# Normalising later, batch-norm coefficients in pieces, and layer 3's norms on GpSimd in a planned four-layer graph network

## The chip, the cores and the metric

The kernel runs on one core of a Trainium2 chip. The metric is the device time of one execution in microseconds (us), taken as the median of several runs. TensorE (PE) multiplies matrices and writes PSUM, VectorE (DVE), ScalarE (ACT) and GpSimd (POOL) do the elementwise work, and SyncE's queue (SP) issues nearly all DMAs.

## The reference

All data are float32. The input x has 128 graphs of 64 nodes with 256 features, and one adjacency matrix serves all graphs. Four layers follow each other, each of the form x = layernorm(x + layer(x)), without gain or bias:

```python
# layer 0: aggregate, linear, batch norm over all rows, relu, linear, batch norm
agg = einsum('nm,bmd->bnd', A_hat, x)
h   = relu(batchnorm(agg @ W1.T + b1, g1, be1))          # 512 channels
out = batchnorm(h @ W2.T + b2, g2, be2)                  # 256 channels
# layer 1: einsum with a scaled Laplacian (power iteration for its largest eigenvalue),
#   @ Wc, layernorm, relu, residual; 4-head masked attention, layernorm; gelu MLP, layernorm
# layer 2: two graph convolutions, then LSTMs over windows of p = 1, 2, 3, 4 nodes,
#   each writing its last hidden state back before the next p
# layer 3: masked graph attention: Wh = x @ W, e = leaky_relu(s1 + s2), softmax, @ Wh
```

A batch norm needs the mean and the variance of each channel over all 8192 rows, so its second half can't begin before the last row of the first half is there. Layer 0 has two such points.

## The kernel before, in words

**Tiles.** The 8192 rows are 16 blocks of 512 rows (128 partitions x 4 tiles `t` of 256 features). `X[i]` holds block i's rows, and `H[i]` holds layer 0's second half of channels and later the LSTM's state. `PS` is a stock of four PSUM tiles of 128x1024, `mem` a stock of eight such tiles in SBUF (`t0` to `t7`), to which `X`, `H` and weight tiles are added when they are free. In the profile a tile's name says which storage a step borrowed, so one step has several names (`t<-`, `x<-`, `h<-`).

**Order.** The order of PE, DVE, ACT and POOL is not left to a scheduler. Each piece of work is a Python generator that yields `step(engine, us, ps, sl, waits, at, tbl)` ahead of the instructions of that step. `flow` keeps a clock for each engine ("T" PE, "V" DVE, "S" ACT, "G" POOL, "Q" the SP queue), and always emits the step that its estimates say can begin soonest; `ps` and `sl` are tiles taken, and `at` is a time before which a step is not ready. A margin, multiplied by a pseudo-random factor that the list `DRAWS` sets for each 50 us of planned time, shifts this choice. Streams hold tasks with a width (how many run at once) and a priority. So the estimates decide nothing about a time on the chip, but they decide every engine's instruction order, and each engine runs its instructions in that order. Steps marked `tbl="m"` on "V" wait in the plan for steps of "G" marked so.

**Layer 0.** `first_block(i)` aggregates a block (line 346), multiplies it by W1 in two halves of channels (`mm_fm`, line 370), lets ACT copy with the bias (line 589) and DVE take the statistics (`bn_stats`, line 593). When all 16 blocks are done, `bn_coeffs` aggregates the four channel groups (line 548), adds eps (549), takes the power -1/2 on POOL (551), and forms scale and shift (553 to 555). `second_block(i)` applies relu(scale*x+shift) on ACT (line 601, four passes a block) and multiplies by W2: block 0 plainly (line 611), the others with a Strassen-like scheme of seven products (line 645), whose sums are on DVE (636, 637, 641, 664 to 669), POOL (639) and ACT (656, 657, 675 to 677). Statistics follow (684), and `bn_coeffs` again.

**From layer 0 to layer 1.** `end_block(i)` loads x again (743), applies the batch norm on ACT (746), transposes on PE (364), adds the residual (DVE, 754), and normalises: `ln_steps_act` takes statistics of each 256-wide tile (`stats`, lines 290 to 292 on DVE), the power on POOL (313), minus mean times scale on DVE (316, `ln_nm`), and applies both with one ACT pass for each tile (319). `block(i)` is layer 1: it aggregates (346), multiplies (382), adds and normalises again (777, then lines 290 to 319), scales and adds (781 to 783 on DVE), transposes (358), and so on. The stream `seq` runs both, six at once; `ends` lists in which order end blocks run, and `at_end` how many of them are queued ahead of which block.

**Layers 2 and 3.** `gcn_block` and `unit` call `lstm`; its products are at lines 1081, 1153, 1289 and 1291, its differences T1 and T4 on POOL (1173, 1201). `last_block` is layer 3: for blocks 0 to 11 a whole block of four tiles, for 12 to 15 two halves of two tiles. It copies the state (1492), transposes, adds (1503), normalises with `ln_steps_act`, transposes (358), multiplies (1532), forms scores (1552 on POOL, 1556, 1557 on PE, 1561 to 1565 on DVE), takes the exponent on ACT (1569), divides (1571, 1572), multiplies (1578, 1588), adds (1599), normalises again with `ln_steps_act`, and stores (1603).

Of the kernel before, what the change touches and what calls it, by code (L numbers as in the profile page):

```python
# [15 lines left out]
P = 128  # L16
# [15 lines left out]
DRAWS = [511, 307, 323, 0, 388, 0, 0, 35, 178, 58, 461, 150, 363, 205, 36, 263, 190, 963, 453, 309, 108, 239, 50, 391, 578, 171, 630, 639, 804, 485, 290, 771, 646, 0, 976, 942, 0, 370, 0, 0, 618, 674, 887, 378, 432, 790, 44, 487, 800, 1]  # L32
# [3 lines left out]
def kernel(ctx: ExitStack, tc: tile.TileContext, a: dict, out: bass.AP):  # L36
# [79 lines left out]
    def mark(*key):  # L116
        done[key] = Clock.end
# [188 lines left out]

    def ln_steps_act(y):
# [6 lines left out]
        yield step("V", 0.2)  # L314
# [96 lines left out]
    with c0:  # L411
# [129 lines left out]
        def bn_coeffs(name, nch, st, g, be):  # L541

            mv = ctile([P, nch, 2], f"{name}mv")
            sc = ctile([P, nch], f"{name}sc")
            sh = ctile([P, nch], f"{name}sh")
            yield step("V", 0.15 + 0.5 * nch)
            for c in range(nch):
                V.bn_aggr(mv[:, c, :], st[:, c, :, :].rearrange("p i s -> p (i s)"))
            V.tensor_scalar(sc, mv[:, :, 1], EPS, None, ALU.add)
            yield step("G", 1.0)  # L550
            G.tensor_tensor(sc, sc, neghalf[:, :nch], ALU.pow)
            yield step("V", 0.6)
            V.tensor_tensor(sc, sc, g, ALU.mult)
            V.tensor_tensor(sh, mv[:, :, 0], sc, ALU.mult)
            V.tensor_tensor(sh, be, sh, ALU.subtract)
            bn[name] = sc, sh
            mark(name)
# [5 lines left out]
        def first_block(i):  # L563
# [6 lines left out]
            yield step("T", 0.95, ps=1, sl=1, tbl="quarter")  # L570
# [23 lines left out]
            mark("l0a", i)  # L594

        def second_block(i):
            sc1, sh1 = bn["bn1"]
# [5 lines left out]
            if i == 0:  # L603
                for f in range(4):
                    yield step("S", 0.7)
                    relu(f)
                    yield step("T", 1.75, ps=int(f == 0), waits=f == 3)
# [16 lines left out]
            yield step("S", 2.92)  # L624
            for f in range(4):
                relu(f)
# [4 lines left out]
            yield step("V", 1.4, sl=2, tbl="m")  # L631
# [5 lines left out]
            V.tensor_tensor(T2, h[:, :, v], T1, ALU.subtract)  # L637
            yield step("G", 1.3, waits=False, tbl="m")
            G.tensor_tensor(T4, h[:, :, u], T2, ALU.subtract)
            yield step("V", 0.7, tbl="m")  # L640
            V.tensor_tensor(T3, h[:, :, v], x[:, :, v], ALU.subtract)
# [8 lines left out]
            yield step("T", 1.75, ps=1)  # L650
# [4 lines left out]
            yield step("S", 0.75, waits=False)  # L655
            S.copy(y[:, 0, :], p[:, 0, :])
            S.copy(y[:, 3, :], p[:, 3, :])
            t = yield step("T", 1.75)
# [11 lines left out]
            yield step("T", 0.88)  # L670
# [3 lines left out]
            yield step("S", 1.5, ps=-1)  # L674
            S.activation(h[:, 0, :], fm(Xs[i])[:, 0, :], AF.Identity, bias=cols["b2"][:, 0:1])
            S.activation(h[:, 1, v], y[:, 3, :], AF.Identity, bias=cols["b2"][:, 1:2])
            S.activation(h[:, 1, u], p[:, 0, :], AF.Identity, bias=cols["b2"][:, 1:2])
# [3 lines left out]
        def second_stats(i):  # L681
            yield step("V", 1.25)
            for c in range(2):
                V.bn_stats(st2[:, c, i, :], H[i][:, c, :])
            mark("l0b", i)
# [4 lines left out]
        tasks.append(  # L690
            (
                lambda: ready(*[("l0a", i) for i in blocks]),
                lambda: bn_coeffs("bn1", 4, st1, cols["g1"], cols["be1"]),
                0,
            )
        )
        tasks += [(lambda: ready(("bn1",)), lambda i=i: second_block(i), 2) for i in blocks]
        tasks.append(
            (
                lambda: ready(*[("l0b", i) for i in blocks]),  # L700
                lambda: bn_coeffs("bn2", 2, st2, cols["g2"], cols["be2"]),
                0,
            )
        )
# [28 lines left out]
    sc2, sh2 = bn["bn2"]  # L733
# [3 lines left out]
    Wv_par = Wv.rearrange("p k (u r e) -> p k r u e", u=2, r=2)  # L737

    def end_block(i):
# [4 lines left out]
        yield step("S", 1.5)  # L744
        for c in range(2):
            S.activation(
                H[i][:, c, :], H[i][:, c, :], AF.Identity, scale=sc2[:, c : c + 1], bias=sh2[:, c : c + 1]
            )
# [8 lines left out]
        yield from ln_steps_act(x)  # L757
        mark("end", i)

    def block(i):  # L760
        x = X[i]
        mark("begun", i)
        yield step("T", 0.95, ps=1, sl=1, tbl="quarter")
# [68 lines left out]
        yield step("T", 0.95, ps=1, sl=1, tbl="quarter")  # L832
# [47 lines left out]
        yield step("T", 0.95, ps=1, sl=1, tbl="quarter")  # L880
# [156 lines left out]
    def lstm(p, n, parts, x_of, out_of):  # L1037
# [7 lines left out]
        us = n * 1.68e-3  # L1045
        v_us, g_us, s_us = (0.08 + n * r for r in (1.15e-3, 2.4e-3, 1.05e-3))
# [43 lines left out]
        def gates(pair, t, ps, sl):  # L1090
            t = yield step("S", 0.1 + n * 2.5e-3, ps=-1, at=t, waits=False)
# [56 lines left out]
        half_us, two_us = (0.15 + j * hn * 1.05e-3 for j in (1, 2))  # L1148
# [13 lines left out]
        for s in range(1, p):  # L1162
# [21 lines left out]
            def stage1(g):  # L1184
# [5 lines left out]
                at[g, "a"] = yield step("S", copy_us, at=t - us, waits=False)  # L1190
# [12 lines left out]
            def stage2(g):  # L1203
                v, y = places(g)
                yield step("T", us, at=h_at, waits=False)
# [8 lines left out]
            def stage3(g):  # L1214
# [3 lines left out]
                at[g, "0"] = yield step("V", two_us, at=at[g], waits=False)  # L1218
# [4 lines left out]
            def stage4(g):  # L1223
# [3 lines left out]
                yield step("S", 0.1 + n * 1.15e-3, at=at[g, "0"], waits=False)  # L1227
# [536 lines left out]
```

## Time and profile before

| | |
|---|---|
| median of 3 runs | 2354.76 us (2354.64 to 2355.97) |
| the profiled execution | 2355.12 us, of which the span is 2353.0 us |
| PE busy | 2266.4 us, 96% of the span |
| DVE, ACT, POOL busy | 58%, 50%, 19% |
| mean granted TensorE clock | 0.987 |
| chain that ended last | PE 80%, issue 8%, DVE 7%, ACT 4% |

The span runs from the first to the last instruction. A matmul in float32 shows as two records, so a product of 512 columns is two records of 0.43 us at the full clock. PEclk is the clock granted to TensorE as a share of the full one; a busy microsecond at 0.5 does half the work. A wait is put down to the instruction that came last before it.

### The profile page before, as it was taken

The page shows a single profiled execution, that of the slowest core. Times are in us where ns is not written, and L with a number is a line of the kernel's source. Part 1 is how long each engine was busy: PE and PEld are TensorE (multiplying, and loading weights), DVE is VectorE, ACT ScalarE, POOL GpSimd, SP SyncE. Part 2 cuts the span into 40 slices and gives each one's busy share as a digit, 9 for nine tenths or more (in the row PEclk, how much of TensorE's full clock was granted, in tenths as well). Part 3 has the DMA queues.
Part 4 walks back from the last instruction along what each step waited for, and adds up shares of the span by engine and source line. Part 5 has one row for each costly group of instructions (what it writes and reads, how often), then busy time and mean ns, then how long its engine had stood idle before and what let it go on. Part 6 is the DMA issues. An engine that isn't in the chain of part 4 may idle for free.

```text
span 2353.0 us, 40443 instructions
## 1 busy us (share of the span) xinstructions
PE 2266.4 (96%) x16916; PEld 1753.1 (75%) x16916; DVE 1365.9 (58%) x2865; ACT 1167.2 (50%) x2257; POOL 435.4 (19%) x322
## 2 busy tenths in 40 slices
PE   8989789999999999999999999999999999999996
PEld 4548666676666676667667888999988888978884
DVE  5557589666766556567544444454454655563567
ACT  2357465644454544445444444444444544653676
POOL 0011124221314224215120100011100111110112
PEclk9999899999999999999999999999999999999998
DMA  6100310000000000101000000000001001000111
GB/s 170 46 1 1 99 60 30 27 10 11 10 10 10 10 11 3 44 2 46 19 19 10 18 1 1 19 1 1 1 1 36 1 10 37 28 10 27 54 37 55
DMA packets 42632, 57.88 MB, mean 25 GB/s; under 512 B 6225, under 2 KB 35537, under 8 KB 42449
## 3 DMA queue, kind: packets, MB, share of 16 engines
q1 hardware_dynamic: 41344, 54.22, 7.2%
q8 instruction: 132, 2.16, 0.4%
q10 hardware_dynamic: 1104, 1.08, 0.1%
q14 instruction: 52, 0.42, 0.1%
HBM read 38.52 MB, written 16.78 MB: 23 GB/s over the span
## 4 chain that ended last, share of the span: by engine, by line
PE 80%; issue 8%; DVE 7%; ACT 4%; POOL 0%; DMA 0%; ACTq 0%; POOLq 0%; DVEq 0%
PE ps L1153 27%; PE ps L1081 14%; PE ps L370 11%; PE ps L382 6%; PE ps L945 4%; PE ps L645 3%; PE ps L346 2%; PE ps L815 2%; PE ps L1532 2%; PE ps L1289 2%; PE ps L1291 2%; PE ps L358 2%; DVE ln_st L290 1%; PE ps L364 1%; DVE ln_mv L291 1%
## 5 line engine op out<-in xcount | busy, mean ns | idle before, releaser
L1153 PE MATMUL ps<-t,x 128*128 128x256 f32 x928 | 226.8, 380 | 0.3 <-DVE x L1221 0.3
L313 POOL TENSOR_TENSOR ln_rs<-ln_rs,neghalf 128x4 f32<-128x4 f32 (+1 forms) x104 | 108.5, 1043 | 610.6 <-DVE ln_rs L292 535.6
L1153 PEld LDWEIGHTS ps<-t,x 128*128 128x128 f32 x928 | 173.0, 190 | 22.8 <-issue 1.6
L1049 ACT ACTIVATE t<-ps,bih 128x512 f32<-128x512 f32 (+5 forms) x185 | 98.2, 568 | 159.7 <-PE ps L1081 103.7
L319 ACT ACTIVATE x<-x,ln_nm,ln_rs 128x256 f32<-128x256 f32 x228 | 118.1, 591 | 66.9 <-DVE ln_nm L316 66.9
L1153 PE MATMUL ps<-x,x 128*128 128x256 f32 x608 | 147.5, 380 | 1.5 <-DVE t L1221 1.1
L1049 ACT ACTIVATE x<-ps,bih 128x512 f32<-128x512 f32 (+5 forms) x159 | 82.2, 548 | 106.3 <-PE ps L1081 67.9
L1153 PEld LDWEIGHTS ps<-x,x 128*128 128x128 f32 x608 | 114.4, 190 | 17.2 <-DVE t L1221 1.8
L370 PE MATMUL ps<-t,W1T 128*128 128x512 f32 x256 | 114.7, 595 | 0.0
L290 DVE BATCH_NORM_STATS2 ln_st<-x 128x6 f32<-128x256 f32 x244 | 97.6, 400 | 0.7
L1049 ACT ACTIVATE x<-x,bih 128x512 f32<-128x512 f32 (+5 forms) x134 | 69.3, 564 | 51.8 <-DVE x L1219 49.7
L1081 PE MATMUL ps<-t,wL 128*128 128x512 f32 x216 | 94.6, 594 | 0.2 <-ACT t L1378 0.2
L291 DVE BATCH_NORM_AGGREGATE ln_mv<-ln_st 128x2 f32<-128x6 f32 x448 | 81.4, 182 | 15.3
L1081 PE MATMUL ps<-h,wL 128*128 128x192 f32 (+2 forms) x456 | 89.6, 352 | 0.6 <-DVE x L1599 0.6
L1081 PE MATMUL ps<-h,x 128*128 128x256 f32 x384 | 86.1, 379 | 0.0
L370 PEld LDWEIGHTS ps<-t,W1T 128*128 128x128 f32 x256 | 46.7, 190 | 48.9 <-issue 48.5
L1081 PEld LDWEIGHTS ps<-h,wL 128*128 128x128 f32 x456 | 69.6, 190 | 17.8 <-issue 16.0
L1212 DVE COPY x<-ps 128x256 f32<-128x256 f32 (+2 forms) x67 | 25.5, 381 | 98.4 <-PE ps L1153 98.4
L1219 DVE TENSOR_TENSOR x<-ps,x 128x512 f32<-128x512 f32 (+2 forms) x67 | 40.8, 609 | 69.3 <-PE ps L1153 64.3
L316 DVE SCALAR_TENSOR_TENSOR ln_nm<-ln_mv,ln_rs 128x4 f32<-128x4 f32 (+1 forms) x104 | 61.4, 593 | 33.2 <-POOL ln_rs L313 33.1
L1081 PEld LDWEIGHTS ps<-h,x 128*128 128x128 f32 x384 | 72.8, 190 | 9.8
L319 ACT ACTIVATE t<-t,ln_nm,ln_rs 128x256 f32<-128x256 f32 x112 | 58.5, 591 | 41.0 <-DVE ln_nm L316 40.9
(692 smaller groups left out, 5374.3 us busy)
## 6 DMA issues: line engine op xcount, KB each, us to landing
t<-in_x_dram SPq DMA_DIRECT2D x28, 512.0 KB, 4.4
xd<-x SPq DMA_DIRECT2D x16, 512.0 KB, 2.6
x<-xd SPq DMA_DIRECT2D x8, 512.0 KB, 3.3
out_dram<-x SPq DMA_DIRECT2D x8, 512.0 KB, 2.9
wL<-in_L_gnn_Wih_dram SPq DMA_DIRECT2D x2, 1024.0 KB, 4.9
x<-in_L_gnn_Whh_dram SPq DMA_DIRECT2D x2, 1024.0 KB, 5.0
wB<-in_L_gnn_W_dram SPq DMA_DIRECT2D x2, 512.0 KB, 4.3
h<-in_x_dram SPq DMA_DIRECT2D x2, 512.0 KB, 4.0
```

Source lines behind the costliest of these rows:

```text
L290: V.bn_stats(st[:, t, :], y[:, t, :])
L291: V.bn_aggr(mv[:, t, :], st[:, t, :])
L313: G.tensor_tensor(rs, rs, neghalf[:, :n], ALU.pow)
L316: V.scalar_tensor_tensor(nm, mv[:, :, 0], -1.0, rs, ALU.mult, ALU.mult)
L319: S.activation(y[:, t, :], y[:, t, :], AF.Identity, scale=rs[:, t : t + 1], bias=nm[:, t : t + 1])
L370: T.matmul(ps[:, c, :], w[:, k, (off + c) * P : (off + c + 1) * P], yT[:, k, :], start=(k == 0), stop=(k == nk - 1),)
L382: T.matmul(ps[:, t, :], yT[:, k, t * P : (t + 1) * P], w[:, k, :], start=(k == 0), stop=(k == nk - 1),)
L645: T.matmul(dst, w[:, k, :], y[:, k, :], start=first and k == 0, stop=k == 1, skip_group_check=not first)
L945: T.matmul(tm(PS[ps])[:, t, :], fm(mem[gs[k // 2]])[:, k % 2, t * P : (t + 1) * P], W2[:, k, :], start=(k == 0), stop=(k == 3),)
L1049: S.activation(dst, z, AF.Tanh, bias=bl[:, p - 1, 2 * g + c : 2 * g + c + 1], scale=(1.0 if g == 2 else 0.5) * (1.0 if p == 1 else 0.5),)
L1081: T.matmul(spread(fm(PS[ps])[:, j, :n], q), WL[p][0][:, k, m], x_of(0, q)[:, k], start=(k == 0), stop=(k == 1),)
L1153: T.matmul(dst, WS[p][name](k, g), y[:, k], start=first and k == 0, stop=k == 1, skip_group_check=not first)
```

## The change

1. **Batch norm in pieces.** `bn_coeffs` works on a range of channel groups. For the first batch norm it is called twice, for groups 0 and 1 (written by the first half of `first_block`) and for groups 2 and 3. Each `bn_aggr` is a step of its own, ready when its group's statistics are complete. Block 0 of `second_block` begins with the first two groups; the other blocks wait for both.
2. **`second_block`** is cut into smaller steps: two relu passes, the difference T1, the first products, two relu passes, the other differences. The last block takes the statistics of its first channel group before its other ACT passes.
3. **Late norms.** `end_block` normalises block 0 alone; for the others the layer norm stands at the beginning of `block(i)`. Four end blocks, not two, are queued ahead of block 0.
4. **True waits on PSUM.** In `lstm` several steps get a later `at` (the time when the tile that they overwrite has been read), and many estimates are changed. `DRAWS` is another list.
5. **Layer 3's norms.** Both use a new `ln_steps_pool`: POOL takes the power, and then applies (y - mean) * rs in one `tensor_scalar` with two scalars of each partition for each tile. Line 316 and the four (or two) ACT passes of line 319 fall away there.

```diff
-DRAWS = [511, 307, 323, 0, ...]
+DRAWS = [438, 839, 188, 0, ...]
...
+    def ln_steps_pool(y):
+        n = y.shape[1]
+        yield step("V", 0.3 + 0.53 * n)
+        mv, rs = stats(y)
+        yield step("G", 1.0)
+        G.tensor_tensor(rs, rs, neghalf[:, :n], ALU.pow)
+        for t in range(n):
+            yield step("G", 0.7, tbl="m")
+            G.tensor_scalar(
+                y[:, t, :], y[:, t, :], mv[:, t, 0:1], rs[:, t : t + 1], ALU.subtract, ALU.mult
+            )
...
+        def bn_coeffs(name, c0, c1, st, g, be, at):
+            sc, sh, mv = (t[:, c0:c1] for t in bn[name])
+            for c in range(c1 - c0):
+                yield step("V", 0.5, at=lambda: at(c0 + c))
+                V.bn_aggr(mv[:, c, :], st[:, c0 + c, :, :].rearrange("p i s -> p (i s)"))
+            yield step("V", 0.2)
             V.tensor_scalar(sc, mv[:, :, 1], EPS, None, ALU.add)
             yield step("G", 1.0)
-            G.tensor_tensor(sc, sc, neghalf[:, :nch], ALU.pow)
+            G.tensor_tensor(sc, sc, neghalf[:, : c1 - c0], ALU.pow)
...
             if i == 0:
                 for f in range(4):
-                    yield step("S", 0.7)
-                    relu(f)
-                    yield step("T", 1.75, ps=int(f == 0), waits=f == 3)
+                    if f % 2 == 0:
+                        for j in (f, f + 1):
+                            t_j = yield step("S", 0.65, at=lambda: done.get(("bn1", f)))
+                            relu(j)
+                    yield step("T", 1.75, ps=int(f == 0), at=t_j - 0.65 * (1 - f % 2))
...
-            yield step("S", 2.92)
-            for f in range(4):
-                relu(f)
+            t_x = yield step("S", 1.46)
+            relu(0)
+            relu(1)
...
+        for c in (0, 2):
+            tasks.append(
+                (
+                    lambda c=c: stats_at(c),
+                    lambda c=c: bn_coeffs("bn1", c, c + 2, st1, cols["g1"], cols["be1"], stats_at),
+                    0,
+                )
...
+    NORMED = range(1)
...
         mem.give(xin)
-        yield from ln_steps_act(x)
+        if i in NORMED:
+            yield from ln_steps_act(x)
         mark("end", i)
...
     def block(i):
         x = X[i]
         mark("begun", i)
+        if i not in NORMED:
+            yield from ln_steps_act(x)
...
-                yield step("T", us, at=h_at, waits=False)
+                yield step("T", us, at=max(h_at, at[g, "a"], at[g, "e"]), waits=False)
                 product(g, "A12", h_u, v[:, 2, :])
...
-        yield from ln_steps_act(x)
+        yield from (ln_steps_pool if True else ln_steps_act)(x)
...
-    at_end = {0: 2, 1: 4, 2: 8, 3: 10, 4: 14, 5: 16}
+    at_end = {0: 4, 1: 4, 2: 8, 3: 10, 4: 14, 5: 16}
```

The line with `ln_steps_pool` stands twice, once for each of layer 3's norms.

## The prediction

> **What bounds the kernel now.** First the page: PE is busy 2266.4 of 2353.0 us, so only its idle time and its time at a reduced clock can be won. Where they lie, the table of stretches says (start:end, the length, busy time with instructions of PE, PEld, DVE, ACT, POOL, then the granted clock):
>
> ```profile
> 0.00:145.00 145.00, 136.34 (x1345) 74.89 (x1346) 75.59 (x159) 39.22 (x61) 2.51 (x15) 1.00 0.32 88
> 145.00:255.00 110.00, 99.49 (x421) 79.89 (x420) 70.90 (x125) 76.86 (x139) 21.35 (x16) 0.97 0.06 19
> 255.00:330.00 75.00, 54.69 (x427) 38.08 (x425) 53.73 (x137) 41.41 (x69) 13.47 (x15) 0.80 0.25 79
> 330.00:400.00 70.00, 66.97 (x744) 49.83 (x743) 58.93 (x120) 42.05 (x64) 33.51 (x19) 1.00 0.12 37
> 400.00:1750.00 1350.00, 1343.95 (x10599) 1018.93 (x10600) 766.63 (x1416) 636.42 (x1098) 283.39 (x171) 1.00 0.04 13
> 1750.00:2000.00 250.00, 238.53 (x1378) 213.42 (x1377) 134.62 (x291) 125.40 (x295) 28.73 (x26) 0.99 0.06 20
> 2000.00:2305.00 305.00, 297.72 (x1761) 258.09 (x1760) 168.44 (x481) 173.59 (x438) 41.62 (x44) 1.00 0.09 30
> 2305.00:2353.00 48.00, 28.73 (x252) 19.96 (x250) 37.02 (x142) 32.22 (x100) 10.81 (x16) 0.80 0.20 66
> ```
>
> Length minus PE busy is the idle time. The same table in slices of 5 us, with busy x (1 - clock) summed, gives what the reduced clock takes: 2.0 us in the second stretch, 9.8 in the third, 1.2 in the sixth, 2.7 in the last. Lost altogether: 8.7 us at the start, 12.5 around the first batch norm, 30.1 around the second, 3.0 and 6.1 in layers 1 and 2, 12.7 and 7.3 in the LSTM with layer 3, 22.0 at the end; 102 in sum. Next the waits of PE in the second and the third stretch (waited for, us, times, longest):
>
> ```profile
> PE ps L611 <- ACT x L601: 6.7, 1, 6.7
> PE ps L358 <- DVE ln_nm L316: 6.3, 1, 6.3
> PE ps L364 <- ACT h L746: 4.9, 2, 4.6
> PE ps L346 <- ACT x L319: 4.1, 1, 4.1
> ```
>
> The first is the first batch norm, the third the second one, the fourth the first layer norm of layer 1, the second a stall 25 us later. Last, in order of time, what stands in the 6.7 us:
>
> ```profile
> 149.90 1.29 DVE L593 BATCH_NORM_STATS2 st<-h 128x6 f32<-128x512 f32 x2 [2.15 <-ACT h L589]
> 151.10 1.91 DVE L548 BATCH_NORM_AGGREGATE bn1mv<-st 128x2 f32<-128x96 f32 x4
> 153.30 1.01 POOL L551 TENSOR_TENSOR bn1sc<-bn1sc,neghalf 128x4 f32<-128x4 f32 x1 [144.18 <-DVE bn1sc L549]
> 155.00 2.22 ACT L601 ACTIVATE x<-x,bn1sh,bn1sc 128x512 f32<-128x512 f32 x3 [4.55 <-DVE bn1sh L555]
> 155.86 5.77 PE L611 MATMUL ps<-x,W2T 128*128 128x512 f32 x8 [6.72 <-ACT x L601]
> ```
>
> PE stood from 149.15 to 155.86, and its next eight records took 5.77 us, where four of the same later take 1.88: the clock was 0.51 in that slice.
>
> **First batch norm.** The last x half has its statistics at 144.3, so groups 0 and 1 can be worked while PE still multiplies the last h halves. Two aggregations (0.48 each) give 145.3, line 549 (0.17) 145.5, POOL's power of 128x2 (0.70, as in the second batch norm) 146.3, three DVE operations 146.9, two relu passes 148.5, between ACT's copies at 145.75 and 149.18. These extra instructions (one line 549, one power, three DVE operations, 1.4 us) lie beside PE's products; without that cover they would cost their 1.4. Block 0's f = 0 and 1 are eight records of 0.43: PE works until 152.6. Groups 2 and 3 end at 151.2, and the same chain reaches the first relu's end at 154.5. The gap shrinks from 6.7 to 1.9 us, -4.8; a gap of 1.9 us at 165 left the clock at 1.00, so the 2.0 us go too. **-6.8.** The finer steps of the other blocks I cost at nothing: PE is bound there (1.03 us for four records, back to back), and the waits left (3.1 us on line 657) stay. Bounds -3 (the early chain queues behind DVE's statistics and ACT's copies, and reaches PE late) and -10 (those waits go too).
>
> **Second batch norm.** One aggregation (0.51 of 1.02 us) leaves the chain: -0.5. Two more end blocks are queued ahead of block 0. Each has two passes of ACT (0.8 each; ACT stands 5.5 us before 275.78), a transposition (3.46 us at half clock in this place, 1.95 at the full one), a DVE sum (1.22) and a load on SP's queue ahead of them; the loads were issued from 245 on. PE waits 4.1 us ahead of 276.44 and 1.1 ahead of 280.39: 5.2 us at half clock, 2.6 us of work that need not be done later. -2.6. Against it, two DVE sums stand ahead of `ln_nm`; they fit while POOL takes the power.
>
> The 6.3 us stall ended at 301.5. Ahead of it DVE did statistics of two later end blocks (292.96 to 297.6, 2.3 us each), then 3.7 us of lines 781 to 783 that PE needs; these were ready at 295.2, when ACT had normalised. With late norms both groups are gone: at least -2.6, and with the two sums of 290.62 already done -3.6; I take -3.1. The clock was at 0.66 from 300 to 315 and cost 4.2 of the 9.8 us; a gap half as long may or may not cause that (2.3 us at 2309.9 did), so half: -2.1. **Sum -8.3**, bounds -3 and -14.
>
> The moved norm brings its nine DVE instructions and `ln_nm`, POOL's power (1.0) and four ACT passes (2.1) to the head of `block(i)`, some 6 us; queued behind the wait on PE is only this block's aggregation, and five other tasks can run. Layers 1 and 2 lose 6.1 us in 1350, with DVE busy 57%, so nothing. If that cover were gone, 15 norms of 6 us would be 90 us, but then these rows would show idle PE. From 330 to 400 DVE is at 84%, and three to four norms leave or arrive there: 0, bounds -2 and +3.
>
> **LSTM and PSUM waits.** No instruction is added; the order is redrawn. 20.0 us are lost from 1750 to 2305, in single waits of at most 1.8 us, mostly on DVE and ACT. Later `at`s keep a product from standing in PE's queue ahead of work that is ready: -2, bounds -8 (half) and +10 (the redrawn order stalls half as much again).
>
> **Layer 3's norms.** 128 ACT passes (66.8 us busy by the table of line 319) and 40 `ln_nm` go; 128 passes come to POOL. No row has such a pass. One input of 256 elements: at least 0.40 (two inputs, 128x128, line 1552), at most 1.36 (two inputs, 128x512, line 639); nearest is 128x256 at 0.62, which I take: 79 us on a POOL that is busy 81 of 603 us. Latency: `ln_nm` 0.16, a hop and two passes of 1.09 against two of 0.62: even. But POOL in turn holds up DVE:
>
> ```profile
> 193.75 0.69 DVE L637 TENSOR_TENSOR t<-h,t 128x512 f32<-128x512 f32 x1
> 195.18 1.54 DVE L637 TENSOR_TENSOR t<-h,t 128x512 f32<-128x512 f32 x1
> 194.61 1.56 POOL L639 TENSOR_TENSOR t<-h,t 128x512 f32<-128x512 f32 x1 [4.50 <-ACT x L656]
> ```
>
> The second DVE sum ends 0.55 us after POOL's at 196.17: it waited. From 2305 on POOL would be busy 10.8 + 28 x 0.62 = 28 of 48 us, and DVE (32.1 of the 36 us from 2310) has 14 such operations (lines 1563 and 1572) and eleven of line 292 (0.25 on average over all 104 of four columns, most of them in layer 1 where POOL works more; 0.17 here): 25 x 0.58 x 0.31 (half a pass) = +4.5, less 2.1 for eleven `ln_nm`: +2.4. ACT loses 14.8 us there, but only part of PE's waits there name it: -1. **End: +1.4**, bounds -3 and, at 1.36, +12. Between 1750 and 2305 the same gives 100 passes, ACT relieved of 52 us, PE's waits on ACT (8.2 us) somewhat shorter and DVE's longer: 0, bounds -3 and +6.
>
> The page "SBUF — State Buffer" of the Trainium skill (section "SBUF: two separate sides") says more: a GpSimd operation and a DVE operation with two SBUF inputs share a port pair as an exclusive lock, and the loser stands for the whole instruction. The row above agrees; by that, with DVE standing for whole passes, the 4.5 would be 9.0, the end +5.9 and the sum -11.2. The page "GPSIMD Engine Reference" (section "Engine selection") speaks against this part: elementwise work belongs on VectorE, though with one input POOL is said to be roughly at line rate. By that, an estimate of 256 / 1.2 GHz = 0.21 us plus dispatch, a pass would lie near the lower bound, the end term near -1 and the sum near -18.
>
> **Sum.** -6.8 - 8.3 - 2 + 1.4 + 0 = -15.7. On the profiled execution's 2355.1 us (the span's 2353.0 and 2.1 around it) that is 2339.4; the median of the runs lies 0.4 lower: **2339 us**. This case's own range, adding up about half of each bound, is 2325 to 2350.
>
> **The rivals.** (a) *The early gain is given back.* The norms come back in 330 to 400, where DVE is at 84%, or the new gaps still reduce the clock: half of the 15.1 us, so 2346. For it: a gap of 2.3 us was enough once. Against: the norms of blocks 12 to 15, four times 2.6 us of DVE, move far away. (b) *The new order loses in the LSTM.* A different list of draws and other estimates reorder all 555 us; the slices of 50 us there range from 0 to 4 us lost. A loss as large again as the 20 now gives 2339 + 22 = 2361 at the worst, 2355 in the middle. Against: the steps now wait for what they really wait for. (c) *POOL becomes the bound of the end: slower.* If a pass costs over about 1.0 us, POOL has 10.8 + 28 = 39 of 48 us, DVE stands behind it, and each half block's two norms grow by 1 us or more. At 1.36: end +12, 1750 to 2305 +6 and T4 on POOL's queue behind passes +3, so 2360; it decides from 1.0 us on. For it: the power takes 0.70 for two elements, so not everything on POOL goes by size. Against: the row at 0.62. (d) *The pieces do nothing*: the order keeps the early coefficients behind the last copies, and the gaps stay: 2351.
>
> **How the numbers follow.** 0.2% (4.7 us) is about what a measurement can tell from no change. Forecast 0.58; (a) 0.12; (b) 0.11; (c) 0.14; (d) 0.05. Faster, below 2350.1: 0.57 + 0.10 + 0.03 + 0.01 + 0.01 = 0.72. Slower, above 2359.5: 0.03 of (b), 0.10 of (c) and 0.03 that several bad bounds meet, taken from forecast and (a): 0.16. The rest, 0.12, lies between. The range from 2325 to 2361 leaves out some 0.05 below, and 0.10 above from (c) and the tail of (b).
>
> **What would show it.** Line 611 starts within 3 us of line 370's last record; no slice there below clock 0.9. The wait on line 316 around 300 is under 4 us; the stretch that begins at the second batch norm loses about 22 us, not 30. POOL's new row has 128 instructions of 0.4 to 0.8 us. The last 48 us lose 19 to 24. A mean above 1 us in that row, or over 25 us lost in the LSTM, would make the prediction wrong.

## The result, and the profile after

The changed kernel takes **2345.34 us**, median of 5 runs (2343.41 to 2348.53), beside 2355.47 us for the kernel before on the same chip (2354.64 to 2355.97): a ratio of 0.9958, interval [0.9944, 0.9973]. It is 10.1 us faster where 16 were forecast. The profiled execution took 2343.84 us, of which the span is 2342.1 us. The time is inside the range, but two terms were wrong and nearly made up for each other.

The table of stretches, in the form shown before (PE, PEld, DVE, ACT, POOL, granted clock):

```profile
145.00:255.00 110.00, 103.77 (x448) 84.07 (x446) 79.46 (x142) 79.79 (x145) 22.38 (x18) 1.00 0.11 36
255.00:330.00 75.00, 61.94 (x767) 47.29 (x768) 49.04 (x108) 43.40 (x63) 15.71 (x15) 0.84 0.22 69
330.00:400.00 70.00, 68.60 (x560) 48.67 (x560) 49.41 (x92) 41.04 (x58) 28.50 (x16) 1.00 0.13 42
400.00:1750.00 1350.00, 1341.26 (x10523) 1024.44 (x10522) 753.41 (x1483) 651.42 (x1130) 287.51 (x176) 1.00 0.03 12
1750.00:2000.00 250.00, 239.68 (x1455) 216.07 (x1454) 134.69 (x308) 118.31 (x287) 72.94 (x61) 1.00 0.07 24
2000.00:2305.00 305.00, 289.39 (x1664) 247.18 (x1662) 167.21 (x460) 134.45 (x361) 139.21 (x123) 0.98 0.09 30
2305.00:2342.00 37.00, 19.71 (x170) 13.19 (x166) 21.49 (x82) 8.57 (x35) 30.28 (x31) 0.72 0.17 58
```

Around the first batch norm PE is idle for 6.2 us where it was 10.5, and the clock stays at 1.00. Around the second one it is idle for 13.1, not 20.3. At the bottom it is the other way round: POOL is now the busiest engine of the last stretch, 30.3 of 37 us, where DVE and ACT led before.

Fixed stretches cut the work of the two kernels at different places, so the ledger goes by milestones: when the last record of a kind starts, in us.

| | before | after | ahead |
|---|---|---|---|
| last product of layer 0 (line 645, now 660) | 262.9 | 251.6 | 11.3 |
| last plain LSTM product (line 1289, now 1322) | 2293.8 | 2273.4 | 20.4 |
| end of the span | 2353.0 | 2342.1 | 10.9 |

Up to the last plain LSTM product more is won than forecast (17.1); then 9.5 of the 20.4 us go in the last 69.

Over the whole span idle time and reduced clock together take 98.1 us, where they took 102.4. So only 4.3 of the 10.9 us were won there. The other 6.6 us are PE's busy time at the full clock, which became shorter with the same 16916 records; no view shows by what (the ends of records are modelled, and the clock is given to two digits). The prediction's opening, that "only its idle time and its time at a reduced clock can be won", does not hold for this profile.

The waits of PE in the first two of the stretches:

```profile
PE ps L377 <- ACT h L775: 5.9, 2, 5.0
PE ps L359 <- ACT x L332: 4.3, 1, 4.3
PE ps L371 <- DVE t L815: 3.3, 1, 3.3
PE ps L628 <- ACT x L616: 2.1, 1, 2.1
```

The last line is the first batch norm (6.7 before), the third the stall 25 us after the second one (6.3 before, then put down to `ln_nm`); the waits of the second batch norm itself have not shrunk (9.0 before in two lines, now 10.2). What stands around the 2.1 us, first on PE and then on ACT, in order of time:

```profile
151.97 3.70 PE L628 MATMUL ps<-x,W2T 128*128 128x512 f32 x8 [2.06 <-ACT x L616]
```

```profile
149.95 1.26 ACT L604 ACTIVATE h<-ps,l0b 128x512 f32<-128x512 f32 x2 [2.17 <-PE ps L383]
151.10 1.51 ACT L616 ACTIVATE x<-x,bn1sh,bn1sc 128x512 f32<-128x512 f32 x2
```

Scale and shift of groups 0 and 1 were ready at 147.6, and ACT then stood idle for 2.17 us, up to 149.95. But in ACT's order the last copies of the first pass (line 604) come ahead of the relu, and so the first product waits for both. Its eight records (two products, f = 0 and 1) take 3.70 us, at the full clock; before they took 5.77. No gap follows, since groups 2 and 3 are ready by 155.5.

In the end the chain of work that ended last runs on POOL (start, length, what):

```profile
2319.32 1.22 POOL h L316
2320.54 0.37 POOL t L1585
2320.91 1.20 POOL h L316
2322.11 1.00 POOL ln_rs L313
...
2324.45 1.22 POOL h L316
...
2327.22 1.21 POOL h L316
2328.43 0.69 POOL ln_rs L313
...
2329.22 2.53 POOL h L316 x2
```

From 2319 to the last pass at 2337.5 POOL goes from pass to power to pass. Its new row, the first of three for line 316, one for each kind of tile (shortest/median/longest in ns, first and last start in us), shows the price of a pass:

```profile
L316 POOL TENSOR_SCALAR x<-x,ln_mv,ln_rs x52: 1212/1220/2507, 1808.3 to 2334.1; 128x256 f32<-128x256 f32 x52
```

A pass takes 1.22 us, and by the groups 1.27 on average, held-up passes included (162.6 us in 128). The forecast took 0.62.

### The profile page after: what moved, and what is told of

Same layout as the page of the kernel before. It is cut to its first block, busy times and chain, and to the rows that moved or that the text cites. A ratio compares the mean times of both kernels' runs of the same rounds, so it can differ in the third digit from the quotient of the medians.

```text
span 2342.1 us, 40447 instructions
## 1 busy us (share of the span) xinstructions
PE 2260.4 (97%) x16916; PEld 1755.7 (75%) x16916; DVE 1330.5 (57%) x2829; ACT 1116.2 (48%) x2137; POOL 599.1 (26%) x451
## 4 chain that ended last, share of the span: by engine, by line
PE 77%; DVE 5%; POOL 3%; ACT 2%; issue 2%; POOLq 0%; DVEq 0%; ACTq 0%
PE ps L1186 26%; PE ps L1114 14%; PE ps L383 11%; PE ps L395 7%; PE ps L977 5%; PE ps L847 2%; PE ps L359 2%; PE ps L371 2%; PE ps L1565 1%; PE ps L1322 1%; PE ps L1324 1%; POOL h L316 1%; DVE ln_st L290 1%; PE ps L920 1%; PE ps L377 1%
## 5 line engine op out<-in xcount | busy, mean ns | idle before, releaser
L1186 PE MATMUL ps<-t,x 128*128 128x256 f32 x800 | 195.0, 380 | 0.0
L1082 ACT ACTIVATE x<-ps,bih 128x512 f32<-128x512 f32 (+5 forms) x201 | 102.9, 547 | 182.4 <-PE ps L1114 106.4
L326 POOL TENSOR_TENSOR ln_rs<-ln_rs,neghalf 128x4 f32<-128x4 f32 x64 | 74.1, 1158 | 432.0 <-DVE ln_rs L292 390.6
L1186 PE MATMUL ps<-x,x 128*128 128x256 f32 x704 | 171.9, 379 | 0.9 <-DVE x L1254 0.9
L1186 PEld LDWEIGHTS ps<-t,x 128*128 128x128 f32 x800 | 150.4, 190 | 20.5 <-issue 1.0
L1082 ACT ACTIVATE t<-ps,bih 128x512 f32<-128x512 f32 (+5 forms) x148 | 78.2, 566 | 136.5 <-PE ps L1114 85.7
L1082 ACT ACTIVATE x<-x,bih 128x256 f32<-128x256 f32 (+5 forms) x146 | 74.1, 558 | 47.9 <-DVE x L1252 47.8
L332 ACT ACTIVATE x<-x,ln_nm,ln_rs 128x256 f32<-128x256 f32 x152 | 78.7, 592 | 33.9 <-DVE ln_nm L329 33.9
L313 POOL TENSOR_TENSOR ln_rs<-ln_rs,neghalf 128x4 f32<-128x4 f32 (+1 forms) x40 | 38.3, 956 | 192.8 <-DVE ln_rs L292 176.8
L1252 DVE TENSOR_TENSOR x<-ps,x 128x512 f32<-128x512 f32 (+2 forms) x73 | 43.7, 600 | 62.5 <-PE ps L1186 55.5
L1114 PEld LDWEIGHTS ps<-t,wL 128*128 128x128 f32 x192 | 36.3, 190 | 44.7 <-issue 42.6
```

Source lines behind the costliest of these rows:

```text
L326: G.tensor_tensor(rs, rs, neghalf[:, :n], ALU.pow)
L332: S.activation(y[:, t, :], y[:, t, :], AF.Identity, scale=rs[:, t : t + 1], bias=nm[:, t : t + 1])
L1082: S.activation(dst, z, AF.Tanh, bias=bl[:, p - 1, 2 * g + c : 2 * g + c + 1], scale=(1.0 if g == 2 else 0.5) * (1.0 if p == 1 else 0.5),)
L1114: T.matmul(spread(fm(PS[ps])[:, j, :n], q), WL[p][0][:, k, m], x_of(0, q)[:, k], start=(k == 0), stop=(k == 1),)
L1186: T.matmul(dst, WS[p][name](k, g), y[:, k], start=first and k == 0, stop=k == 1, skip_group_check=not first)
```

## The experiments

Three questions: what POOL's passes cost and where; what each half of layer 0's change is worth; and what the new order alone does. One theory says that the end's loss of 9.5 us is POOL's long pass, its rival that it is the redrawn order. One thing stands in the way: whatever changes a step makes the plan draw every later choice anew. Six kernels therefore keep a planned order (the steps are announced as before, only the instructions behind them differ; PE's order is the same record by record), and the rest were planned anew. Beside all of them the kernel before took 2354.9 to 2355.2 us, so their times can be set beside the 2345.34 of the changed kernel.

### Which engine applies layer 3's norms

**Passes on ACT, planned anew** (`act`):

```diff
-        yield from (ln_steps_pool if True else ln_steps_act)(x)
+        yield from ln_steps_act(x)
```

> The changed kernel with layer 3's two norms applied by ACT again (ln_steps_act), all else as changed. Theory 1 (a POOL pass of 1.2 us makes POOL the bound of the end): the last 48 us lose about 22 us as before, not 37 to 41 us over the last 90, and the time is 2333 to 2338 us. Theory 2 (the end is longer because the whole order was redrawn, not because of POOL): 2343 to 2348 us, with the end as long as in the changed kernel.

Measured: 2333.23 us (2332.36 to 2333.97), ratio 0.9906 [0.9893, 0.992]. It beats both kernels: with layer 3's norms left on ACT, the rest of the change, in the order that came out of this plan, is worth 22 us. On PE the order is that of the changed kernel up to 1810 us.

**The changed kernel's order, passes on ACT** (`order_pool_act`):

```diff
         for t in range(n):
             yield step("G", 0.7, tbl="m")
-            G.tensor_scalar(
-                y[:, t, :], y[:, t, :], mv[:, t, 0:1], rs[:, t : t + 1], ALU.subtract, ALU.mult
-            )
+            if t == 0:
+                nm = sm.tile([P, n], F32, tag="ln_nm", name="ln_nm")
+                V.scalar_tensor_tensor(nm, mv[:, :, 0], -1.0, rs, ALU.mult, ALU.mult)
+            S.activation(
+                y[:, t, :], y[:, t, :], AF.Identity, scale=rs[:, t : t + 1], bias=nm[:, t : t + 1]
+            )
```

> The order of every engine as the changed kernel has it (the same planned steps), but in layer 3's norms the passes are emitted on ACT, with line 316's old product on DVE ahead of them. Only the engine differs. Theory 1 (POOL's passes of 1.2 us themselves cost the end): 2333 to 2338 us, 8 to 12 less than the changed kernel. Theory 2 (the order planned for POOL costs it): 2343 to 2347 us.

Measured: 2336.72 us (2335.62 to 2338.23), ratio 0.9923 [0.9909, 0.9937].

**`act`'s order, passes on POOL** (`order_act_pool`): the same exchange the other way round.

```diff
...
+        yield step("V", 0.2, tbl="m")
+        yield step("S", 0.1 + 0.5 * n)
+        for t in range(n):
+            G.tensor_scalar(
+                y[:, t, :], y[:, t, :], mv[:, t, 0:1], rs[:, t : t + 1], ALU.subtract, ALU.mult
             )
...
-        yield from (ln_steps_pool if True else ln_steps_act)(x)
+        yield from ln_steps_act_pool(x)
...
```

> The order of the kernel that had ACT do the norms in the changed plan (2333 us), but the passes are emitted on POOL. Theory 1: 2343 to 2350 us, 10 to 16 more. Theory 2 (it is the order): 2333 to 2336 us.

Measured: 2360.37 us (2357.5 to 2361.88), ratio 1.002 [1.0011, 1.0029]. That is 10 us above the dearer of the two theories; why POOL costs so much more in this order is not shown. The four together:

| | passes on POOL | passes on ACT | POOL costs |
|---|---|---|---|
| order planned for POOL | 2345.34 | 2336.72 | 8.6 |
| order planned for ACT | 2360.37 | 2333.23 | 27.1 |

In either order POOL is the slower place. In its own order it costs 8.6 us, and that is the exchange of the engine alone. Where in the span, the two profiles with the same order show; each row is the stretch from the last plain LSTM product to the end, first of the changed kernel, then of `order_pool_act`:

```profile
2273.40:2342.10 68.70, 42.34 (x310) 30.20 (x308) 41.66 (x147) 22.48 (x81) 51.76 (x50) 0.77 0.14 47
```

```profile
2271.70:2334.20 62.50, 43.51 (x310) 29.51 (x308) 42.43 (x159) 37.86 (x111) 12.58 (x18) 0.79 0.15 51
```

The same 310 records of PE stand behind the milestone in both. With POOL they take 68.7 us, with ACT 62.5: 6.2 of the spans' 7.9 us are lost here, the rest before. POOL is the busiest engine of its stretch (51.8 of 68.7 us), while with ACT no engine is above 43.5 of 62.5.

**Half blocks on ACT, whole blocks on POOL, same order** (`halves_act`):

```diff
-            G.tensor_scalar(
-                y[:, t, :], y[:, t, :], mv[:, t, 0:1], rs[:, t : t + 1], ALU.subtract, ALU.mult
+            if n == NT:
+                G.tensor_scalar(
+                    y[:, t, :], y[:, t, :], mv[:, t, 0:1], rs[:, t : t + 1], ALU.subtract, ALU.mult
+                )
+                continue
+            if t == 0:
+                nm = sm.tile([P, n], F32, tag="ln_nm", name="ln_nm")
+                V.scalar_tensor_tensor(nm, mv[:, :, 0], -1.0, rs, ALU.mult, ALU.mult)
+            S.activation(
+                y[:, t, :], y[:, t, :], AF.Identity, scale=rs[:, t : t + 1], bias=nm[:, t : t + 1]
             )
```

> The changed kernel's order, with layer 3's passes on POOL for the whole blocks and on ACT for the half blocks of the end. All passes on ACT in this order took 2336.7, all on POOL 2345.3. If the cost of POOL's long pass lies in the half blocks of the end, as the critical chain of the last 25 us says: 2336 to 2340. If the whole blocks cost as much (layer 3 before 2270, where the last LSTM product is within 2 us of the other order's): 2342 to 2346.

Measured: 2339.23 us (2337.87 to 2341.25), ratio 0.993 [0.9918, 0.9943]. Taking 32 of 128 passes off POOL gives back 6.1 of the 8.6 us. The half blocks of the end carry most of the cost, as the chain said; how the remaining 2.5 us are shared can't be read within these intervals.

**Two cheaper kinds of pass on POOL, same order** (`kinds`): the first norm's pass leaves out the mean, and the second norm's leaves out mean and scale and uses two constants, so this kernel does not work out the layer; it shows only what the passes cost.

```diff
...
+            G.tensor_scalar(
+                y[:, t, :], y[:, t, :], rs[:, t : t + 1], None, ALU.mult
+            )
...
+            G.tensor_scalar(
+                y[:, t, :], y[:, t, :], 0.5, 2.0, ALU.subtract, ALU.mult
             )
...
-        yield from (ln_steps_pool if True else ln_steps_act)(x)
+        yield from ln_steps_one(x)
...
-        yield from (ln_steps_pool if True else ln_steps_act)(x)
+        yield from ln_steps_imm(x)
...
```

> The changed kernel's order and engines, with the passes of layer 3 in two cheaper kinds: the first norm's pass only multiplies by one scalar per partition (the mean is not subtracted), the second norm's subtracts 0.5 and multiplies by 2.0, both constants (its statistics and power are made and not used by the pass). Computation is changed in these two places alone. The pass of the changed kernel, with two operations and two scalars per partition, takes 1.22 to 1.27 us where 0.62 was assumed. If a pass is paid by operations on each element: the first norm's about 0.6 to 0.65 us, the second's about 1.2. If it is paid for fetching the scalars per partition: the second's 0.4 to 0.6, the first's about 0.9. If by elements alone: all 1.2. The whole time goes down towards 2336 in as far as the passes get shorter, as with the passes on ACT in the same order.

Measured: 2336.15 us in one run. Its passes, from the answers for the two lines (316 is one operation with one scalar for each partition, 329 two operations with constants):

```profile
L316 POOL TENSOR_SCALAR x<-x,ln_rs x26: 920/929/1923, 1810.1 to 2298.9; 128x256 f32<-128x256 f32 x26
...
L329 POOL TENSOR_SCALAR x<-x x26: 1064/1070/1661, 1871.3 to 2326.4; 128x256 f32<-128x256 f32 x26
```

Neither theory is right alone. Against the 1.22 us of the changed kernel, dropping the second operation and one scalar saves 0.29, dropping both scalars 0.15. If these add up, a scalar of each partition costs 0.075, the second operation 0.22, and 0.85 remain for a pass with one operation and no such scalar (an estimate from three medians); the multiplication of two 128x256 inputs (line 1585) takes 0.62. By that estimate what the forecast lacked is mostly in the remainder: this instruction form is dear on POOL whatever its scalars. With passes of 0.99 and 1.07 on average (63.3 and 68.4 us for 64 each) the time is down to what ACT gives: by this one run, nearly all of the 8.6 us come from the last 0.2 us or so of a pass.

### What layer 0's pieces are worth

**Coefficients all together, planned anew** (`whole`): the kernel before's `bn_coeffs` and `second_block` in the changed kernel.

```diff
-            for c in range(c1 - c0):
-                yield step("V", 0.5, at=lambda: at(c0 + c))
-                V.bn_aggr(mv[:, c, :], st[:, c0 + c, :, :].rearrange("p i s -> p (i s)"))
+            yield step("V", 0.15 + 0.5 * nch)
+            for c in range(nch):
+                V.bn_aggr(mv[:, c, :], st[:, c, :, :].rearrange("p i s -> p (i s)"))
```

> The changed kernel with layer 0's batch norm in one piece and second_block as before. Theory 1 (the pieces are worth the gap, the clock after it and the waits of the second pass): the gap ahead of line 611 is 6.7 us again, the second pass takes about 107 us, not 100, and the time is 2353 to 2357 us. Theory 2 (later work is bound otherwise and takes the gain back): 2345 to 2348 us.

Measured: 2410.77 us, ratio 1.0222 [1.0207, 1.0238]. A miss by 55 us, and the whole time gives no answer: only 12.6 us have gone by the end of layer 0 (264.2, after 251.6), while the last plain LSTM product starts 74 us later than in the changed kernel. The draws met another plan. In layer 0 itself the run does answer. The gap ahead of block 0's first product is 6.72 us again, PE waits 6.9 us in the products behind it, and from the last record of the first pass to the last product of the second one it is 115.1 us, with the changed kernel's list of draws. So the shorter second pass comes with layer 0's new steps, and not from the list alone.

**Coefficients all together, order kept** (`whole_fixed`): groups 0 and 1 wait for groups 2 and 3, and block 0's products are all issued late.

```diff
+            held = name == "bn1" and c0 == 0
...
-            V.tensor_scalar(sc, mv[:, :, 1], EPS, None, ALU.add)
+            if not held:
+                V.tensor_scalar(sc, mv[:, :, 1], EPS, None, ALU.add)
...
-                            relu(j)
+                            for k in [] if f == 0 else (0, 1, 2) if j == 2 else (3,):
+                                relu(k)
```

> The changed kernel's plan and the order of every matmul in it kept, but the first batch norm's coefficients are all worked out together, once the last groups' statistics are there, and block 0's products follow them. Theory 1 (the pieces are worth the gap and the clock after it): the gap ahead of block 0's first product is 6.5 to 7 us with a reduced clock behind it, and the time is 6 to 9 us above the changed kernel, 2351 to 2355 us. Theory 2 (later work takes it back): 2345 to 2348 us.

Measured: 2349.7 us (2348.14 to 2351.01), ratio 0.9979 [0.997, 0.9987], 4.4 us over the changed kernel, between the two theories. In PE's order of time the old gap is back to the hundredth, and four records take 3.78 us (1.90 in the changed kernel; the granted clock is 0.50 from 155 to 160):

```profile
154.83 3.78 PE L636 MATMUL ps<-x,W2T 128*128 128x512 f32 x4 [6.72 <-ACT x L622]
```

From the last record of the first pass to the last product of the second one it is 113.75 us before, 108.1 here and 101.7 after. So the pieces are worth 6.4 us, of which this kernel's whole time shows 4.4; in its profile the first pass happened to end 1.8 us sooner. The other 5.65 us come from what this kernel keeps: the finer steps of `second_block`, its new estimates and the order drawn from them, which no run separates. In the waits of PE within these products, first before and then after, they show as 4.4 us, 5.5 against 1.1:

```profile
PE ps L645 <- ACT x L657: 3.1, 2, 1.9
PE ps L645 <- DVE x L669: 1.9, 3, 1.2
PE ps L645 <- DVE x L664: 0.5, 1, 0.5
```

```profile
PE ps L660 <- ACT x L678: 0.9, 1, 0.9
PE ps L660 <- DVE x L690: 0.2, 1, 0.2
```

### What the late norms are worth

**All norms with the end blocks, planned anew** (`early`):

```diff
-    NORMED = range(1)
+    NORMED = range(16)
...
-    at_end = {0: 4, 1: 4, 2: 8, 3: 10, 4: 14, 5: 16}
+    at_end = {0: 2, 1: 4, 2: 8, 3: 10, 4: 14, 5: 16}
```

> The changed kernel with every end block normalising its own rows again and two end blocks queued ahead of block 0 (NORMED = range(16), at_end 0: 2). Theory 1 (late norms are worth about 3 us of DVE time ahead of layer 1's first transposition and of PE's clock there): PE's first transposition of line 371 starts 3 to 5 us later against the last record of layer 0's second pass than in the changed kernel (37.6 us after it), and the time is 2347 to 2351 us. Theory 2 (what is won there is given back): the start is later, but the time is 2344 to 2346 us.

Measured: 2396.56 us, ratio 1.0177 [1.0163, 1.0191]. Again the whole time is a miss, 51 us over the changed kernel in an order that was drawn anew behind 260 us. Up to there PE's order is the same, and the last product of layer 0 starts within 0.3 us of the changed kernel's, so the place where the change acts can be compared. From 255 to 330 it loses 28.5 us (idle and reduced clock), the changed kernel 21.2: 7.3 of the 51 us. The stall of the kernel before is back, with the same releaser:

```profile
PE ps L371 <- DVE ln_nm L329: 6.4, 1, 6.4
```

The first transposition itself starts only 1.8 us later against the last product of layer 0 (39.8 us, 38.0 in the changed kernel), less than the 3 to 5 expected: the changed kernel has PE do more of later blocks' work ahead of it.

**Norms with the end blocks, order kept** (`early_fixed`): statistics, power and passes move back to the end blocks, PE's order stays.

```diff
...
+        else:
+            apply_pending()
+            mv, rs = stats(x)
+            G.tensor_tensor(rs, rs, neghalf, ALU.pow)
+            pending.append((i, x, mv, rs))
...
```

> The changed kernel's plan and the order of every matmul in it kept, but each end block's layer norm is emitted with the end block (statistics and power at once, the product and the ACT passes ahead of the next end block's statistics) and not at the head of its block. Only DVE, ACT and POOL get that work early. Theory 1 (late norms keep DVE free ahead of layer 1's first transposition): the first record of line 371's transposition is 3 to 5 us later and the time is 2348 to 2351 us. Theory 2 (the gain is given back where the norms return): 2344 to 2347 us.

Measured: 2383.92 us (2380.16 to 2387.73), ratio 1.0128 [1.0113, 1.0144]: 38.6 us lost where 3 to 6 were expected. The waits of PE from 255 to 400:

```profile
PE ps L371 <- DVE t L838: 15.9, 2, 10.1
PE ps L359 <- ACT x L332: 11.7, 1, 11.7
```

Line 838 is the scaled sum of layer 1 (815 in the changed kernel, where it is waited for 3.3 us). With the statistics of the later end blocks ahead of it in DVE's queue, layer 1's first transposition starts at 303.7, not 289.6. So norms that nothing needs yet do stand in the way of what PE needs, as the prediction read from the 6.3 us stall. The size is likely too large: an order of PE that was drawn for late norms is here given early ones. In their own place the late norms are worth about 7 us by `early`; what is left of that at the end of the kernel no run tells.

### What the order does

**Norms on POOL in the kernel before** (`before_pool`): its order is the old one up to about 1830 us, and then drawn anew. `ln_steps_pool` is added as in the change, and the line stands twice.

```diff
...
-        yield from ln_steps_act(x)
+        yield from ln_steps_pool(x)
...
```

> The kernel before with nothing changed but layer 3's two norms applied by POOL in one pass. Theory 1: the same passes of about 1.2 us fill POOL at the end, the end grows by 7 to 12 us, 2362 to 2368 us. Theory 2 (POOL costs nothing by itself): 2354 to 2357 us.

Measured: 2395.53 us, ratio 1.0172 [1.0158, 1.0186], 40 us over the kernel before and far above both theories. Its last plain LSTM product starts at 2295.4, 1.6 us later; everything else is lost behind it (first the kernel before, then this one):

```profile
2293.80:2353.00 59.20, 39.93 (x314) 29.09 (x312) 43.63 (x163) 37.58 (x111) 13.04 (x19) 0.84 0.16 54
2295.40:2392.20 96.80, 58.35 (x398) 42.40 (x396) 52.20 (x182) 30.93 (x102) 71.93 (x70) 0.76 0.12 41
```

The kernel before has 314 records of PE behind that point and needs 59.2 us. Here 398 are left, and POOL is busy 71.9 of 96.8 us. Two things go together here, and the run doesn't separate them: POOL's passes, and more of layer 3 left to a time when no LSTM product fills PE's idle time.

**`act` with the list of draws of the kernel before** (`act_draws`):

```diff
-DRAWS = [438, 839, 188, 0, ...]
+DRAWS = [511, 307, 323, 0, ...]
```

> Layer 3's norms on ACT as in the fastest kernel so far (2333), planned with the list of draws of the kernel before in place of the changed kernel's. If a list of draws fits only the plan that it came with, and the redrawn kernels lost their 40 to 65 us to that: 2360 to 2395. If the draws matter little and those kernels lost it to POOL's passes planned too short: 2330 to 2340.

Measured: 2353.74 us (2350.53 to 2355.96), ratio 0.9991 [0.9982, 1.0]: 20.5 us more than `act`, by the list alone and without a pass on POOL. The last plain product starts at 2268.7 (`act` 2267.9); 446 records are left there (314), and they take 85.5 us (62.4). It lies between the two expectations: this one list, which wasn't found for the plan, costs some 20 us, not 40 to 65.

**A true duration for POOL's pass** (`plan`):

```diff
-            yield step("G", 0.7, tbl="m")
+            yield step("G", 1.25, tbl="m")
```

> The changed kernel with a duration of 1.25 us for POOL's pass in the plan, where it has 0.7 and the trace shows 1.27; the order is drawn again from about 1790 us on. If the false duration is what spoils the order: 2334 to 2342. If the list of draws fits only the plan that it came with: 2350 to 2385.

Measured: 2355.8 us (2353.55 to 2356.67), ratio 1.0002 [0.9993, 1.0011], 10.5 us more than with the false 0.7; the end takes 77.7 us with 322 records. Knowing the pass better did not help; that the list of draws met another plan is the likely reason, but with the passes still on POOL the run doesn't show it by itself.

## Why the prediction was right, and where it wasn't

**First batch norm: right in size, not in place.** -6.8 was forecast and 6.4 shown. The gap left over is 2.06 us against 1.9. The working put it behind block 0's first products, which it let start at 149.15 with the coefficients of 146.9; in fact these products wait, since ACT's order has the last copies first, and the second gap isn't there. That a gap of nearly the same length stands at another place is luck. The failed step is "between ACT's copies at 145.75 and 149.18". The coefficients were in time: they were there at 147.6, in a profile whose first pass ends 0.8 us later, and ACT stood idle from 147.78 to 149.95. The order put the relu passes behind the last copies all the same.

**The finer steps of `second_block`: wrong.** "I cost at nothing", with "the waits left (3.1 us on line 657) stay". They went from 5.5 to 1.1 us, and the second pass became shorter by 5.65. The bound of -10 had named this; "PE is bound there" was no reason to price them at nothing, with 5.5 us of waits on record in these products. Of the 5.65, the 1.2 that the waits don't show stay open (records' ends are modelled).

**Second batch norm and late norms: right direction, size not settled.** From the last product of layer 0 to the last plain LSTM product 9.1 us were won, against 8.3 + 2 forecast. Counted from that last product of layer 0, idle time and reduced clock go from 28.1 to 24.1 us in the first 67 us and from 3.0 to 1.7 in the 70 us after: -5.3. From 400 to 1750, where most of the moved norms run and the forecast put nothing, idle time grew by 2.65 us, from 6.07 to 8.72; with the LSTM's -1.7 that makes -4.3, and the other 4.8 of the 9.1 us are the shorter busy time of PE, which stays open. The stall at 300 shrank from 6.3 to 3.3 us (-3.1 forecast), and with the norms back at the end blocks (`early`) it is 6.4. But the stretch's reduced clock went down by 1.7 rather than 2.1 (the 4.2 us from which that half was taken are 3.7 in slices of 5 us), and the waits of the second batch norm itself, from which "-2.6" for two more end blocks should have come, did not shrink.

**Returned norms from 330 to 400, LSTM: right.** No idle time came back from 330 to 400. From 1750 up to the last plain product the loss (idle and clock) is 18.3 us, before 20.0: -1.7, against -2; whether the later `at`s did it, the estimates or the list, no run shows. By the prediction's own words over 25 us lost in the LSTM would speak against it; to 2305 it is 30.7, but behind 2275 no plain LSTM product is left, and the excess is the end's, begun 20 us sooner.

**Layer 3's norms: the wrong term.** +1.4 was forecast for the end, +9.5 came: 68.7 us behind the last plain product against 59.2. Of these 6.2 are the engine (same order, 68.7 against 62.5), and 3.3 the order and what it left for the end. The step that failed is the price of a pass: "nearest is 128x256 at 0.62, which I take". That row has the number of elements, but another instruction form; the pass costs 1.22, near the upper bound of 1.36. "A mean above 1 us in that row" was named as what would make the prediction wrong, and it is 1.27; the last 48 us lose 27.7 us, not the 19 to 24 named. The way of the loss was also another: the sum priced DVE held up by POOL. In the same order DVE's instructions other than `ln_nm`, from 1790 us on, take 339.3 us with POOL's passes and 331.2 with ACT's, 8.1 us more, while 11.9 us of `ln_nm` fall away. Behind the last plain LSTM product it is 47.0 against 46.3 us for the same 147 instructions: 0.7 us, where the sum had +4.5. In the last 20 us it is POOL's own queue that the chain runs through.

**The rivals.** (c) was the right mechanism, though for POOL's own chain more than for a DVE that "stands behind it", and its "from 1.0 us on" fits: at 1.27 us a pass costs 8.6, at about 1.03 (`kinds`, one run) next to nothing. It priced itself at 21 us, which is too much in this order, and what layer 0 gave besides hid it. (b)'s mechanism was seen with another list (`act_draws`, 20.5 us), and the kernels planned anew came out 10 to 65 us over the changed one, with other causes among them; in the order that came with the change it was not. Of (a) there is little: the 2.7 us more idle time from 400 to 1750, which no run ties to the norms. (d) had the order right in part, since ACT's relu passes do stand behind the last copies; but the gap closed to 2.06 us all the same, because the coefficients were ready when the copies ended.

The ledger closes: -15.7 forecast, -5.65 for the finer steps, +8.1 for the end, +1.2 for what lies between layer 0 and the last plain product (-9.1 for -10.3), +0.4 for the first batch norm, and +0.8 for a first pass that ended later than in the profile before (149.91 for 149.15) make -10.9, the difference of the two spans. Two errors of opposite sign did most of it, and that the time lies so near the forecast is in part their luck.

**A rule weighed.** For one input the Trainium skill ("GPSIMD Engine Reference", section "Engine selection") says that it runs roughly at line rate; the estimate of 0.21 us and dispatch worked out from it is far off for this form: 0.93 with one operation, 1.22 with two. With its advice to do elementwise work elsewhere the runs agree, though it names VectorE: on ACT the pass takes 0.59 us, and the kernel is 8.6 us faster in the same order.

## What to carry to other kernels

Price a new operation by rows of its own instruction form; the size of the tile alone misled by a factor of two, and where rows are lacking, a bound near which a rival decides deserves more chance than the nearest row suggests. An engine with spare time over the whole span isn't spare in the last stage: count its passes on the chain of the last items, and move those back first. Where an order is drawn for one plan, test a part with the order held fixed; a kernel planned anew can be read up to the place where its order parts from the other's, but its whole time can't. PE's busy time is no fixed sum either: in this pair of profiles it gave more than half of the gain.

## What the runs showed of the hardware

- POOL takes longer for one input with scalars than for two inputs of the same size: 1.22 us (two operations, two scalars of each partition), 1.07 (two operations, constants) and 0.93 (one operation, one scalar) against 0.62 for a product of two 128x256 tiles.
- POOL's passes hold DVE up, but little here: in layer 3 DVE's line 292 on 128x4 took 0.249 us on average (24 times) against 0.171 in the same order with the passes on ACT. POOL's 128 passes took 6.4 us more than 128 times their median (162.6 - 128 x 1.22); that DVE is the reason is not shown.
- A gap of 2.06 us at 150 left the clock at 1.00; the gap of 6.72 us of `whole_fixed` in the same place is followed by a clock of 0.50.
